# Third layer's end: the four sequences' ends in skewed stages, silu(z) loaded during the scan, x kept in DRAM, and the fourth layer's weights turned between the stages

## The chip, the cores and the metric

The kernel runs on one core of a Trainium2 chip. The core has five engines that work side by side, each on its own queue of instructions in order: TensorE (PE, matrix products, with a second queue PEld for loading the stationary operand), VectorE (DVE), ScalarE (ACT), GpSimd (POOL), and SyncE (SP), which here only starts DMA transfers. An engine waits for another through semaphores. On-chip memory is SBUF (128 partitions) and PSUM (where products land); DRAM is reached by DMA. The metric is the device time of one execution in microseconds, as the median of several runs.

## The reference

The program is a network of four different layers over an input of 4 sequences x 1024 tokens x 128 channels, all in one kernel. Every layer is of the form

```
xn = layernorm(x)
s  = mixer(xn)              # differs per layer
g  = silu(ffn(xn))          # differs per layer
x  = x + s * g
```

The change is at the end of the third layer and the start of the fourth. The third layer's mixer is a gated delta-rule scan with 16 heads. It makes from xn the projections z, x_gate, K and V, from a convolution of x_gate seven gates and the queries, and runs a recurrence over time. What follows the recurrence is this:

```
retrieved = einsum('blhsd,blhd->blhs', Y, Q) * sel_C_gate   # 16 heads x 2
y  = retrieved.reshape(b, l, 32) @ readout_w                # 32 -> 256
yf = y.reshape(b, l, 16, 16)                                # 16 groups of 16 channels
mean, var over (l, 16 channels of the group)                # group norm over all of a sequence
y  = (yf - mean) * rsqrt(var + 1e-5) * gn_w + gn_b
y  = y * silu(z)
y  = y + D_param * x_conv
out = residual + y @ out_w                                  # 256 -> 128
```

Its ffn is a mixture of eight experts. The fourth layer's mixer is causal attention with 16 heads of width 8 and relative position embeddings (`(q k + skewed(q e)) / sqrt(8)`, softmax, times v, `@ Wp.T + bp`), and its ffn is a SwiGLU with int8 weights divided by 127.

## The kernel before

**Frame.** x lives in one SBUF tile, `x_all` (128 tokens by partition, 4 x 8 tiles of tokens, 128 channels), from the first layer to the end of the third. `layer2` (L929-992; layers count from 0, so this is the third) writes the new x of each sequence to a DRAM tile `x3`, from which `layer3`, the fourth, reads.

**Third layer.** `norm(b)` normalises a sequence of x_all and stores it to DRAM (`xd`, L958). `project2` makes the projections; silu(z) goes to DRAM (`szd`), the residual with the D term already multiplied by out_w (`rd`) too, and the gate g of the experts (`gd`). `scan2` (L1382-1521) runs the recurrence in chunks. It is one stream of 64 steps on DVE with work of other kinds between the steps: `chunks2` makes four tables (`ktd`, `kdd`), one for each quarter of the steps, and each quarter fetches its part again from DRAM (`ktc`, `kdc`, `kt`, `qt`, L1297 and L1467-1469); the experts' work is interleaved with `next(beside)`.

**Its end.** `retrieve2` (L1523-1540) makes the transposed `retT`, 32 rows for each sequence. Then a loop goes over the four sequences (L983-992). For each: load silu(z), g and rd (L985-989), `out2`, then the update and the store. `out2` (L1542-1585): four products `py` of 32 rows by 512 columns (L1553), each copied to `y` by ACT (L1554), with DVE's statistics (L1555, L1556); two small products `pm` with a matrix of group means (L1563, L1567) with small DVE operations between (L1562-1566), a square root on ACT and four small DVE operations (L1570-1574); y scaled and shifted on DVE (L1576) and multiplied by silu(z) on POOL (L1577), 1024 columns at a time; 16 output products for each sequence in the program, 32 instructions in the trace (`po`, L1583), and two additions of `resid` on DVE (L1585). `k.update` (L225-228) then multiplies resid by g and adds it to x_all, both on POOL, for a whole sequence at once, and L992 stores the sequence to x3. Most tiles here have two buffers, so that the next sequence's loads and py products start while the current one ends.

**Fourth layer's start.** `load3` (L1602-1616) loads the weights; `prepare3` (L1628-1666) turns them: transposes of Wq, Wk, Wv, four transposes of a widened Wp with 16 DVE pieces (`WpB`, L1639-1644), eight transposes of the padded relative embeddings (`pad`, `emb`, L1650-1661), and the dequantised FFN weights (L1664). All of this stands in the program after the third layer and before `layer3` (L1672 on). `layer3` begins with sequence 0 alone: eight loads from x3 (L1809), layernorm (L136-143), transposes (L1824), products for q, k, v, and then a long pipeline of units in which scores, softmax and values of one unit lie between those of others. The scheduler is none other than the order of the program: each engine executes its instructions as written, and waits are put in from the tiles' uses.

## Time and profile before

| | us |
|---|---|
| median of 3 runs | 3265.0 (3252.33 to 3279.71) |
| profiled execution, device time | 3261.59 |
| its span | 3259.9 |
| mean granted TensorE clock | 0.734 of full speed |

The profiled execution is 3.4 us below the median; its span is 1.7 us shorter than its time. All times below are in microseconds from the span's start of that one execution. Where the stages lie:

| stage | from - to |
|---|---|
| last update of x by the second layer ends | 1277.1 |
| first store of normalised x (L958) | 1285.0 |
| first step of the scan | 1662 |
| fourth table's store leaves (L1378) | 1813.3 |
| loads of the last quarter's `ktc` leave (L1467, L1468) | 1826.8 - 1829.2 |
| last quarter of the scan begins | 1865 |
| last step of the scan | 2037 |
| first py product of sequence 0 | 2067.7 |
| last addition of resid, sequence 3, ends | 2153.5 |
| x3 store of sequence 3 leaves | 2158.8 |
| first load of the fourth layer leaves | 2161.6 |
| first normalisation in the fourth layer (L138) | 2168.3 |
| first comparison of scores in the fourth layer (L1986) | 2194.2 |
| end | 3259.9 |

The page gives each engine's busy time and count, then the span in 40 slices with busy tenths, the granted TensorE clock and the DMA traffic, and then groups of instructions by source line. A group's row has the busy time, the mean of one, the idle time of the engine just before, and what released it. The window rows cut the same data by stretches of time. In the timeline, a line has start, length, engine, source line, operation, tiles, shape and count, and in brackets the engine's idle time before it and who ended it. Rows with `q` behind the engine's name (SPq) are of its sequencer.

### The profile page before, as it was taken

Reading aid. Unit: us, or ns where it says so; the run is one execution under the profiler, and the core shown is the slowest. Engines: PE = TensorE matmul, PEld = TensorE weight load, DVE = VectorE, ACT = ScalarE, POOL = GpSimd, SP = SyncE. Lnnn points to the kernel's source line nnn. Section 1 sums busy time; section 2 is a strip of 40 time slices with the busy share of each in tenths; the row PEclk is TensorE's granted clock in tenths of the full one; section 3 lists DMA queues with packets and bytes.
Section 4 is the critical chain, followed back from the end, with each engine's and each line's share of the span. In section 5 each row is a group of like instructions: output and inputs, shape, how many; then the busy total and the mean of one; then the engine's idle time right before and its main releaser. Section 6 shows DMA issues by size and latency. Waiting matters only on the chain. (4 is left out here: it accounts for less than half of the span.)

```text
span 3259.9 us, 50636 instructions
## 1 busy us (share of the span) xinstructions
PE 2317.2 (71%) x18321; PEld 1327.2 (41%) x18321; DVE 2307.1 (71%) x5534; ACT 1487.5 (46%) x3248; POOL 1174.5 (36%) x1104
## 2 busy tenths in 40 slices
PE   5787777677776777965533772557888888888885
PEld 2555555222322323651101222344545555555553
DVE  5555545878878886657868878437678778777786
ACT  4555453433333334344322561125665665755663
POOL 3344334144444444224577222332322322323322
PEclk9888888678788888985555666566766766756676
DMA  3000000100000000320433444347677677766772
GB/s 89 3 1 1 1 1 1 35 0 0 0 0 1 0 0 33 105 84 0 111 95 105 109 108 99 110 119 209 187 213 207 181 209 217 202 195 193 200 231 71
DMA packets 396446, 303.46 MB, mean 93 GB/s; under 512 B 96272, under 2 KB 380812, under 8 KB 390564
## 3 DMA queue, kind: packets, MB, share of 16 engines
q1 hardware_dynamic: 395044, 296.03, 32.2%
q10 hardware_dynamic: 1152, 4.19, 0.4%
q8 instruction: 144, 2.36, 0.3%
q14 instruction: 106, 0.87, 0.1%
HBM read 160.63 MB, written 138.94 MB: 92 GB/s over the span
## 5 line engine op out<-in xcount | busy, mean ns | idle before, releaser
L2000 ACT ACTIVATE neg<-neg,low 128x640 f32<-128x640 f32 (+7 forms) x512 | 390.0, 763 | 153.9 <-DVE low L1993 153.8
L1945 POOL TENSOR_SCALAR_AFFINE_SELECT rel<-rel 128x512 f32<-128x512 f32 x288 | 179.9, 637 | 565.6 <-DMA rel<-flat 357.3
L1737 DVE STREAM_TRANSPOSE wT<-neg 128x640 f32<-128x640 f32 (+7 forms) x512 | 362.0, 753 | 7.6 <-ACT neg L2000 6.9
L1978 PE MATMUL score<-k,q 8*128 8x512 f32 (+3 forms) x1536 | 295.0, 747 | 91.2 <-DVE low L1993 91.0
L1993 DVE CUSTOM_DVE_ANT_0 neg<-score,rel,low 128x128 f32<-128x128 f32 (+3 forms) x448 | 217.5, 516 | 152.5 <-PE score L1978 105.6
L1914 PE MATMUL pr<-emb,q 8*128 8x256 f32 x1024 | 245.2, 569 | 45.0 <-ACT r L1916 27.2
L2014 PEld LDWEIGHTS po<-wT,vb 128*32 128x32 f32 x10240 | 208.1, 140 | 143.3 <-issue 78.0
L2014 PE MATMUL po<-wT,vb 128*32 128x64 f32 (+1 forms) x10240 | 242.9, 259 | 31.7 <-issue 17.3
L1914 PEld LDWEIGHTS pr<-emb,q 8*128 8x128 f32 x1024 | 153.6, 269 | 124.4 <-ACT r L1916 62.9
L1916 ACT COPY r<-pr 128x512 f32<-128x512 f32 x256 | 138.4, 581 | 144.2 <-PE pr L1914 95.1
L1993 DVE CUSTOM_DVE_ANT_0 neg<-score,rel 128x512 f32<-128x512 f32 (+3 forms) x320 | 149.3, 520 | 26.7 <-issue 15.4
L1978 PEld LDWEIGHTS score<-k,q 8*128 8x128 f32 x1536 | 103.0, 249 | 153.9 <-DVE low L1993 127.8
L835 PE MATMUL pg<-xnT,w 128*128 128x512 f32 x256 | 148.4, 663 | 7.7 <-DVE h L839 4.5
L214 PE MATMUL pt<-ident,three 128*24 128x128 bf16 x64 | 9.2, 295 | 201.9 <-DVE three L211 201.9
L788 POOL TENSOR_TENSOR prod<-rest,kv 128x2048 f32<-128x2048 f32 x32 | 145.6, 4599 | 18.4 <-ACT rest L778 18.4
L837 PE MATMUL pu<-xin,w 128*128 128x512 f32 x256 | 140.5, 632 | 14.3 <-DVE h L839 7.9
L826 PE MATMUL po<-h,w 128*128 128x512 f32 x256 | 129.6, 627 | 27.1 <-DVE h L839 27.1
L838 ACT ACTIVATE h<-pg 128x512 f32<-128x512 f32 x128 | 75.9, 595 | 156.2 <-PE pg L835 152.7
L1986 DVE TENSOR_SCALAR_CACHE_REDUCE neg<-score 128x384 f32<-128x384 f32 (+2 forms) x192 | 79.7, 415 | 69.3 <-PE score L1978 69.3
L1050 PE MATMUL ph<-xin,upT 128*128 128x512 bf16 (+1 forms) x128 | 71.3, 588 | 78.5 <-DVE xin L1044 77.7
L1455 PE MATMUL read<-kt,const_sb 128*128 128x128 f32 x256 | 50.1, 366 | 94.2 <-POOL kt L1450 94.2
L431 PE MATMUL px<-hT,xbcT 128*128 128x512 f32 x256 | 115.4, 595 | 0.0
(621 smaller groups left out, 5690.5 us busy)
## 6 DMA issues: line engine op xcount, KB each, us to landing
flat<-r SPq DMA_DIRECT2D x256, 256.0 KB
rel<-flat SPq DMA_DIRECT2D x112, 512.0 KB
flat<-r SPq DMA_DIRECT2D x256, 128.0 KB
rel<-flat SPq DMA_DIRECT2D x96, 256.0 KB
kt<-kd SPq DMA_DIRECT2D x16, 512.0 KB
qt<-qd SPq DMA_DIRECT2D x16, 512.0 KB
kdc<-kdd SPq DMA_DIRECT2D x16, 512.0 KB
ktc<-ktd SPq DMA_DIRECT2D x16, 512.0 KB
```

Source lines behind the costliest of these rows:

```text
L788: nc.gpsimd.tensor_tensor(prod, attn.rearrange("p (t h g) -> p t h g", t=4, g=16)[:, t].unsqueeze(2).to_broadcast(each), kv[:, t, 1, :].re ...
L826: nc.tensor.matmul(po, W["w2"][:, e, c, :], h[:, c, :], start=(e == 0 and c == 0), stop=(e == 7 and c == 1))
L835: nc.tensor.matmul(pg, W["w1"][:, e, c * P : (c + 1) * P], xnT, start=True, stop=True)
L837: nc.tensor.matmul(pu, W["w3"][:, e, c * P : (c + 1) * P], xin, start=True, stop=True)
L1737: nc.vector.transpose(weights[at, pair][j][:, t % 2, 0 : (t + 1) * P], S[j][:, 0 : (t + 1) * P])
L1914: nc.tensor.matmul(to[:, m, :], q[at, t * P : (t + 1) * P], W["emb"][at, i, :], start=True, stop=True)
L1916: nc.scalar.copy(r[:, n], to)
L1945: nc.gpsimd.affine_select(out=rel[:, :, slot(back), :], in_=rel[:, :, slot(0), :], compare_op=op, fill=fill, base=0, pattern=[[0, 4], [-si ...
L1978: nc.tensor.matmul(sc[:, j, 0 : last - first], q[at(j), 1 + t * P : 1 + n], kk[at(j), first:last], start=True, stop=True)
L1993: nc.vector.tensor_tensor_reduce(out=neg[:, begin:last], in0=sc[:, j, begin - first : last - first], in1=rel[:, j, slot : slot + (last - b ...
L2000: nc.scalar.activation(neg[:, 0:n], neg[:, 0:n], AF.Exp, bias=here, scale=-1.0, accum_out=group["sums"][:, j, t : t + 1])
L2014: nc.tensor.matmul(o[32 * j : 32 * j + 32, 2 * pair + m.start : 2 * pair + 2, :], vb[:, kb, j].rearrange("p a d -> p (a d)"), weights[j][: ...
```

## The change

The end of the third layer is rewritten, and four things are moved.

- **x by way of DRAM.** `norm(b)` also stores x_all to a new DRAM tile `xr`. After the gates are made, x_all's room is given up (`whole.close()`), and a pool for the fourth layer's turned weights is opened in its place. Each sequence's end loads its x from xr into one of two buffers.
- **silu(z) during the scan.** The tiles of `chunks2` are in pools of their own. Once the four tables are made, `behind_tables()` closes these, opens a pool with four silu(z) tiles in their room, and issues their loads (1 MB each) on SP.
- **The ends in stages.** The loads of resid and g for all four sequences, and of the fourth layer's weights, stand ahead of `retrieve2`. `out2` is a generator with four stages: py and statistics; group statistics; scaling, product with silu(z), load of x; output products, additions, update and store. A loop runs them skewed: in round n sequence b is at stage n - b, for sequence 0 first.
- **Weights turned between.** `prepare3` is a generator too, and one of its steps follows each stage.
- **Engines.** Scaling y goes from DVE to ACT; the product with silu(z) for the second 128 of the 256 channels from POOL to DVE; resid times g from POOL to DVE. The addition to x stays on POOL. Both go by half a sequence now, and so does the store to x3.

The order of instructions in `layer3` is unchanged on every engine. The diff:

```diff
--- before.py
+++ after.py
@@ -926,14 +926,17 @@
     nc.scalar.activation(W["ldt"], W["ldt"], AF.Exp)
 
 
-def layer2(k, W, x_all, eps5, ps, banks, x3):
+def layer2(k, W, x_all, eps5, ps, banks, x3, whole, last, I):
 
     nc, tc = k.nc, k.tc
     tokens = lambda b: slice(b * NT, (b + 1) * NT)
     with tc.tile_pool(name="l2", bufs=1) as keep, tc.tile_pool(name="l2dram", bufs=1, space=DRAM) as dram:
         wide = lambda name: dram.tile([P, NB * NT, D], F32, tag=name, name=name)
 
-        xd, rd, gd = wide("xd"), wide("rd"), wide("gd")
+        xd, rd, gd, xr = wide("xd"), wide("rd"), wide("gd"), wide("xr")
         szd = dram.tile([P, 2, NB * T], F32, tag="szd", name="szd")
 
         kd = dram.tile([NT, NB, 16, 16, P], F32, tag="kd", name="kd")
@@ -954,6 +957,7 @@
 
                 def norm(b):
 
+                    nc.sync.dma_start(out=xr[:, tokens(b), :], in_=x_all[:, tokens(b), :])
                     var, rs = k.layernorm(p2, x_all[:, tokens(b), :], xn[:, tokens(b), :], eps5)
                     nc.sync.dma_start(out=xd[:, tokens(b), :], in_=xn[:, tokens(b), :])
                     ms = p2.tile([P, NT], F32, tag="ms", name="ms")
@@ -972,24 +976,48 @@
             experts = experts2(k, W, f1, f2, ps, xd, gd)
             with tc.tile_pool(name="l2m", bufs=1) as mp:
                 gates2(k, W, mp, ps, raw, cosp, sinp, outg, coef, experts)
+        whole.close()
+        t3 = last.enter_context(tc.tile_pool(name="t3", bufs=1, side="right"))
+        room, szs = ExitStack(), []
+        tp1 = room.enter_context(tc.tile_pool(name="l2t", bufs=1, side="right"))
+        tp2 = room.enter_context(tc.tile_pool(name="l2td", bufs=2, side="right"))
+        def behind_tables():
+            room.close()
+            pre = room.enter_context(tc.tile_pool(name="l2pre", bufs=1, side="right"))
+            for b in range(NB):
+                szs.append(pre.tile([P, 2, T], F32, tag=f"sz{b}", name="sz"))
+                nc.sync.dma_start(out=szs[b], in_=szd[:, :, b * T : (b + 1) * T])
         with late, tc.tile_pool(name="l2s1", bufs=1) as p1, tc.tile_pool(name="l2s", bufs=2) as p2, \
                 tc.tile_pool(name="l2sd", bufs=2, space=DRAM) as dram2:
-            scan2(k, p1, p2, ps, dram2, kd, qd, coef, o, experts)
+            scan2(k, p1, p2, ps, dram2, kd, qd, coef, o, experts, tp1, tp2, behind_tables)
         banks.close()
         ps = PsumTags(banks, tc, {"mm": 4, "tr": 2, "o": 2}, "ps2o")
-        with tc.tile_pool(name="l2o", bufs=2) as p2:
-            retT = p2.tile([P, T], F32, tag="retT", name="retT")
-            retrieve2(k, p2, ps, o, cosp, sinp, outg, retT)
+        with room, tc.tile_pool(name="l2o", bufs=NB) as p4, tc.tile_pool(name="l2x", bufs=2) as p2, \
+                tc.tile_pool(name="l2r", bufs=1) as p1, tc.tile_pool(name="w3", bufs=1) as w3:
+            parts = []
             for b in range(NB):
-                sz = p2.tile([P, 2, T], F32, tag="szb", name="szb")
-                nc.sync.dma_start(out=sz, in_=szd[:, :, b * T : (b + 1) * T])
-                g = p2.tile([P, NT, D], F32, tag="g", name="g")
+                resid, g = (p4.tile([P, NT, D], F32, tag=tag, name=tag) for tag in ("resid", "g"))
+                nc.sync.dma_start(out=resid, in_=rd[:, tokens(b), :])
                 nc.sync.dma_start(out=g, in_=gd[:, tokens(b), :])
-                resid = p2.tile([P, NT, D], F32, tag="resid", name="resid")
-                nc.sync.dma_start(out=resid, in_=rd[:, tokens(b), :])
-                out2(k, W, p2, ps, b, retT, sz, resid, eps5)
-                k.update(x_all[:, tokens(b), :], resid, g)
-                nc.sync.dma_start(out=x3[:, tokens(b), :], in_=x_all[:, tokens(b), :])
+                parts.append((resid, g))
+            W3 = load3(k, w3, I)
+            turned = prepare3(k, t3, W3, ps)
+            retT = p1.tile([P, T], F32, tag="retT", name="retT")
+            retrieve2(k, p1, ps, o, cosp, sinp, outg, retT)
+            ends = [
+                out2(k, W, p4, p2, ps, b, retT, szs[b], *parts[b], eps5, xr[:, tokens(b), :], x3[:, tokens(b), :])
+                for b in range(NB)
+            ]
+            for n in range(2 * NB):
+                for b in range(NB):
+                    if 0 <= n - b:
+                        next(ends[b], None)
+                        next(turned, None)
+            drain(turned)
+        return W3
 
 
 def experts2(k, W, p1, p2, ps, xd, gd):
@@ -1379,7 +1407,7 @@
         yield ktd, kdd
 
 
-def scan2(k, p1, p2, ps, dram, kd, qd, coef, o, beside):
+def scan2(k, p1, p2, ps, dram, kd, qd, coef, o, beside, tp1, tp2, behind_tables):
 
 
 
@@ -1387,7 +1415,7 @@
     nc = k.nc
     v = nc.vector
     whole = p1.tile([P, 512 // CH], F32, tag="whole", name="whole")
-    tables = chunks2(k, p1, p2, ps, dram, kd, coef, whole)
+    tables = chunks2(k, tp1, tp2, ps, dram, kd, coef, whole)
     made = []
 
     def table():
@@ -1515,6 +1543,9 @@
                     table()
             while c == NC - 6 and len(made) < min(4, i + 2):
                 table()
+            if behind_tables and len(made) == 4:
+                behind_tables()
+                behind_tables = None
     for i in (NT - 2, NT - 1):
         drain(made_of[i])
     drain(beside)
@@ -1539,7 +1570,7 @@
     k.transpose_tiles(ps, "tr", tiles, retT)
 
 
-def out2(k, W, p2, ps, b, retT, sz, resid, eps5):
+def out2(k, W, p2, px, ps, b, retT, sz, resid, g, eps5, x_from, x_to):
 
     nc = k.nc
     y = p2.tile([P, 2, T], F32, tag="y", name="y")
@@ -1554,6 +1585,7 @@
             nc.scalar.copy(y[:, c, tok], py)
             nc.vector.bn_stats(st[:, c, half, :], y[:, c, tok])
         nc.vector.bn_aggr(mv[:, c, :], st[:, c])
+    yield
     mean, var = mv[:, :, 0], mv[:, :, 1]
     pm = ps.tile([P, 4], F32, tag="o", name="pm")
     flat = p2.tile([P, 4], F32, tag="flat", name="flat")
@@ -1572,17 +1604,26 @@
     nc.vector.tensor_tensor(scale, scale, W["gnw"], ALU.mult)
     nc.vector.tensor_tensor(shift, scale, pm[:, 0:2], ALU.mult)
     nc.vector.tensor_tensor(shift, W["gnb"], shift, ALU.subtract)
+    yield
     for c in range(2):
-        nc.vector.tensor_scalar(y[:, c, :], y[:, c, :], scale[:, c : c + 1], shift[:, c : c + 1], op0=ALU.mult, op1=ALU.add)
-        nc.gpsimd.tensor_tensor(y[:, c, :], y[:, c, :], sz[:, c, :], ALU.mult)
+        nc.scalar.activation(y[:, c, :], y[:, c, :], AF.Identity, bias=shift[:, c : c + 1], scale=scale[:, c : c + 1])
+    nc.gpsimd.tensor_tensor(y[:, 0, :], y[:, 0, :], sz[:, 0, :], ALU.mult)
+    nc.vector.tensor_tensor(y[:, 1, :], y[:, 1, :], sz[:, 1, :], ALU.mult)
+    x = px.tile([P, NT, D], F32, tag="x", name="x")
+    nc.sync.dma_start(out=x, in_=x_from)
+    yield
     for half in range(2):
         po = ps.tile([P, 4, D], F32, tag="o", name="po")
         for t in range(4):
             at = (4 * half + t) * P
             for c in range(2):
                 nc.tensor.matmul(po[:, t, :], y[:, c, at : at + P], W["outw"][:, c, :], start=(c == 0), stop=(c == 1))
-        r = resid[:, 4 * half : 4 * half + 4, :]
-        nc.vector.tensor_tensor(r, r, po, ALU.add)
+        part = slice(4 * half, 4 * half + 4)
+        nc.vector.tensor_tensor(resid[:, part], resid[:, part], po, ALU.add)
+        nc.vector.tensor_tensor(resid[:, part], resid[:, part], g[:, part], ALU.mult)
+        nc.gpsimd.tensor_tensor(x[:, part], x[:, part], resid[:, part], ALU.add)
+        nc.sync.dma_start(out=x_to[:, part], in_=x[:, part])
+    yield
 
 
 
@@ -1626,11 +1667,13 @@
 
 
 def prepare3(k, w, W, ps):
     nc = k.nc
     new = lambda name, shape: w.tile(shape, F32, tag=name, name=name)
     for name in ("Wq", "Wk", "Wv"):
         W[name + "T"] = new(name + "T", [P, D])
         k.transpose_tiles(ps, "tr", [W[name]], W[name + "T"])
+        yield
 
     W["WpB"] = new("WpB", [P, 4, 4, D])
     with k.tc.tile_pool(name="wide3", bufs=1) as rp:
@@ -1642,6 +1685,7 @@
             nc.tensor.transpose(pt, wide[:, i].rearrange("p j a d -> p (j a d)"), k.ident)
             for a in range(4):
                 nc.vector.tensor_scalar(W["WpB"][:, i, a, :], pt, k.c("of_a")[:, a : a + 1], None, op0=ALU.mult)
+            yield
     W["bpw"] = new("bpw", [P, D])
     nc.gpsimd.tensor_copy(W["bpw"], W["bp"])
     W["emb"] = new("emb", [P, 4, 256])
@@ -1653,6 +1697,7 @@
                 nc.gpsimd.tensor_copy(spread(pad[:, c, :])[:, i], heads_of(W["rel"][:, c, :])[:, i])
         for i in range(4):
             k.transpose_tiles(ps, "tr", [pad[:, c, i * P : (i + 1) * P] for c in (0, 1)], W["emb"][:, i, :])
+            yield
 
         e0 = rp.tile([P, 4], F32, tag="e0", name="e0")
         nc.vector.tensor_copy(e0, W["emb"][:, :, 0])
@@ -1664,6 +1709,7 @@
             nc.vector.tensor_scalar(f, W[name], 1.0 / 127.0, None, op0=ALU.mult)
             W[name + "T"] = new(name + "T", [P, 3, D])
             k.transpose_tiles(ps, "tr", [f[:, c, :] for c in range(3)], W[name + "T"].rearrange("p c d -> p (c d)"))
+            yield
 
 
 ORDER3 = (7, 0, 6, 1, 5, 2, 4, 3)
@@ -2087,7 +2133,7 @@
     xp = whole.enter_context(tc.tile_pool(name="x", bufs=1, side="right"))
     x_all = xp.tile([P, NB * NT, D], F32, tag="x_all", name="x_all")
 
-    right = ExitStack()
+    right, last = ExitStack(), ExitStack()
     w1 = right.enter_context(tc.tile_pool(name="w1", bufs=1, side="right"))
     with tc.tile_pool(name="w0", bufs=1) as w0, ExitStack() as st:
         ps = PsumTags(st, tc, {"mm": 4, "tr": 2, "o": 2}, "ps0")
@@ -2113,14 +2159,9 @@
             st2 = ExitStack()
             ps = PsumTags(st2, tc, {"mm": 4, "tr": 2, "o": 2}, "ps2")
         with st2:
-            layer2(k, W2, x_all, eps5, ps, st2, x3)
-    w3 = right.enter_context(tc.tile_pool(name="w3", bufs=1, side="right"))
-    W3 = load3(k, w3, I)
-    with whole, right, tc.tile_pool(name="t3", bufs=1) as t3, ExitStack() as st:
+            W3 = layer2(k, W2, x_all, eps5, ps, st2, x3, whole, last, I)
+    with last, ExitStack() as st:
         ps = PsumTags(st, tc, {"sc": 1, "tr": 3, "o": 1}, "ps3")
-        prepare3(k, t3, W3, ps)
-        right.close()
-        whole.close()
         layer3(k, W3, x3, out, eps5, ps)
 
 
```

## The prediction

> **What bounds the kernel now.** I read the page first. TensorE and VectorE are equally loaded over the whole span, and neither is full, so the page alone decides nothing about one stage.
>
> ```profile
> PE 2317.2 (71%) x18321; PEld 1327.2 (41%) x18321; DVE 2307.1 (71%) x5534; ACT 1487.5 (46%) x3248; POOL 1174.5 (36%) x1104
> PEclk9888888678788888985555666566766766756676
> ```
>
> One slice is 81.5 us. The change lies in slices 26 and 27, where the granted clock is 0.5 to 0.6. Next I cut that time into stages: last scan reads and loads; the four sequences' ends (L1542-1585); the update of x and the turning of layer 3's weights; layer 3's start; layer 3's bulk.
>
> ```profile
> 2050.00:2068.00 18.00, 9.55 (x49) 8.82 (x50) 6.77 (x8) 1.44 (x3) 4.57 (x3) 0.69 0.84 292
> 2068.00:2153.00 85.00, 53.59 (x176) 37.23 (x175) 36.44 (x73) 10.93 (x21) 34.40 (x15) 0.57 0.21 68
> 2153.00:2166.00 13.00, 5.55 (x24) 4.15 (x24) 9.94 (x34) 1.66 (x5) 7.90 (x18) 0.74 0.24 78
> 2166.00:2209.00 43.00, 28.01 (x104) 18.59 (x104) 3.46 (x23) 18.20 (x34) 8.69 (x8) 0.61 0.78 216
> ```
>
> Columns: PE, PEld, DVE, ACT, POOL busy, clock, DMA share, GB/s. In the second row no engine is full: 53.6 us of PE in 85. The waits of that stretch say why:
>
> ```profile
> PEld po L1583 <- POOL y L1577: 22.9, 8, 6.0
> PE po L1583 <- POOL y L1577: 18.4, 8, 5.9
> PEld pm L1567 <- DVE flat L1566: 14.2, 4, 5.6
> ```
>
> PE idles in each sequence for its statistics and for its product with silu(z), because each sequence ends before the next gets through. Third sequence, in order of time:
>
> ```profile
> 2120.29 0.58 PE L1567 MATMUL pm<-flat,const_sb 128*128 128x2 f32 x2 [5.52 <-DVE flat L1566]
> 2123.70 4.99 POOL L1577 TENSOR_TENSOR y<-y,szb 128x1024 f32<-128x1024 f32 x2 [3.47 <-DVE y L1576]
> 2128.74 6.24 PE L1583 MATMUL po<-outw,y 128*128 128x128 f32 x28 [1.08 <-POOL y L1577]
> 2135.01 0.69 DVE L1585 TENSOR_TENSOR resid<-resid,po 128x512 f32<-128x512 f32 x1 [2.14 <-PE po L1583]
> 2135.78 2.34 POOL L227 TENSOR_TENSOR resid<-resid,g 128x1024 f32<-128x1024 f32 x1 [7.10 <-DVE dev L1564]
> 2135.80 2.33 DVE L1565 TENSOR_TENSOR dev<-dev 128x2 f32<-128x2 f32 x1
> ```
>
> The last two lines matter: a DVE product of 128x2 takes 2.33 us beside POOL's product, and 0.16 us alone (least of that row), ending with POOL's. The sequences' last residual additions end at 2095.27, 2115.38, 2135.70 and 2153.47: 20.1, 20.3 and 17.8 us apart, 85.8 us from the first py matmul (2067.65). Then the way into layer 3:
>
> ```profile
> 2154.00 2.35 POOL L227 TENSOR_TENSOR resid<-resid,g 128x1024 f32<-128x1024 f32 x1
> 2156.43 2.34 POOL L228 TENSOR_TENSOR x_all<-x_all,resid 128x1024 f32<-128x1024 f32 x1
> 2161.56 3.65 SPq L1809 DMA_DIRECT2D x<-x  x8
> 2168.29 0.30 ACT L138 ACTIVATE ln_rs<-ln_mv,eps 128x8 f32<-128x8 f32 x1 [3.41 <-DVE ln_mv L137]
> ```
>
> From 2153.47 to the first normalisation of layer 3 at 2168.29 there are 14.8 us, in which nothing but POOL's update, the store, eight loads and the weights' turning happens. The weights' turning runs beside them, so the chain is the update's.
>
> **The change, part by part.**
>
> *The ends in stages.* I add PE's own work in the new order, as the built kernel has it. All 16 py products stand ahead of the first output product. Here 12 of them took 9.06+2.07+5.48 = 16.6 us, 1.38 each, so 16 take 22.1. Four pairs of pm at 0.58 add 2.3, and the turnings of Wq, Wk, Wv and of four wide tiles 2.1 (seven at about 0.3). The first output product comes 26.5 us after the first py (before: 18.8). After it come 128 output products (28.6 us in the window), pads' and FFN weights' transposes (2.2 + 2.4), four pm pairs (2.3) and the last residual addition (0.7). PE's sum is 62.7 us. Above it stand the waits that staging does not cover. Last sequence alone, from second pm to output product, was 5.6 us in the third sequence; in the new order the third sequence's output products (7.15 us) lie beside it. The uncovered part is 0 if every small DVE operation is alone, and about 9 if one of them in each sequence waits out a POOL product (4 x 2.2). I take the middle, 4.5: in the row of before three of four waited, but then POOL's products were twice as long. The stage takes 67.2 us instead of 85.8: 18.6 less, bounds 14 to 23.
>
> *Moves between engines in it.* y's scaling goes from DVE (two of 0.77) to ACT. ACT was busy 10.9 of 85 us and a copy of 128x512 took 0.59, so two of about 1.1; the first lies on the chain with +0.3, taken as part of the 4.5. One half of y times silu(z) goes from POOL (2.5) to DVE (1024 columns, twice the 0.68 of L1537: 1.3), parallel to POOL's half, and resid times g from POOL (2.34) to DVE (two of 0.68). DVE gains 4 x (1.3 + 1.4 - 1.5) = 4.8 us on 36.4 + 9.9; it has 67, so it stays below. If it stops being covered, that is 5 us.
>
> *The way into layer 3.* New: resid times g 0.68, x plus resid of half a sequence on POOL 1.17, store 0.32, three load issues 1.3 (five stand in front of the last store, and they no longer wait for its landing, since only the first sequence is read), and from the last issue's end to ln_rs 3.1 as before. That is 6.6, plus 1 for one DVE product behind a POOL one: 7.5 (6.6 to 9). It was 14.8: 7.3 less. What now waits in a queue: on DVE a sequence's residual additions (for its output products) stand ahead of the next one's product with silu(z), which is in the order summed above; on SP the third x load waits, and only later stores and layer 3's loads are behind it. The turning (9.9 us of DVE, 5.5 of PE) goes into the stage above and is in its sum.
>
> *x by DRAM.* Four stores of 512 KB ahead of the first normalised x's store. x was complete at 1277.1, that store left at 1285.0, and DMA moved 1 GB/s between: nothing on the path. If that cover were gone, four times 512 KB at the 223 GB/s shown below, 9 us. Four loads on SP: the third and fourth wait for the store of the sequence two before, 20 us ahead of their use: nothing, else one landing (2 to 3 us) each.
>
> *silu(z) during the scan.* Four loads, 4.2 MB, on SP ahead of the ktc loads of the scan's fourth block. The ktc loads left at 1826.8 to 1829.2; the block starts near 1865, and DMA stood still from 1840 to 1850:
>
> ```profile
> 1840.00:1850.00 10.00, 9.90 (x19) 2.34 (x19) 8.66 (x26) 8.78 (x19) 1.42 (x2) 0.60 0.00 0
> 1857.00:1866.00 9.00, 3.08 (x27) 2.89 (x26) 7.41 (x28) 1.42 (x5) 3.59 (x3) 0.95 1.03 223
> ```
>
> At 223 GB/s they take 19 us, and 2.1 MB of ktc 9 more: from 1818 to about 1846, some 15 us early. Cost 0; bounds -1 (the z loads gone from 2051) and +20: if all of it leaves only at 1829 and runs at half the rate, ktc is there at 1885. At 2051 the same 4.2 MB leave as before (eight loads of resid and gate instead of two sequences' z, gate and resid), so layer 3's weights behind them come no later.
>
> *Sum.* 18.6 + 7.3 = 25.9. Layer 3's instructions keep their order, so the earlier start is passed on. From the profiled execution's 3261.6 us: 3235.7. The median of the three runs is 3.4 above that execution, so I set 3237.
>
> **The rivals.**
>
> *DVE behind POOL.* Twelve products with two SBUF operands move to DVE, and POOL's remaining 12 run beside them. If each waits out a POOL operation, 12 x 2.2 = 26 us, of which 4.5 are in the sum: 22 of the 26 us come back, 3258. For it: 3 of the 4 L1565 took over 0.2 us. Against: POOL gives up 4 x (2.5 + 2.3) us of 34. The same result comes if all py and the turnings, ahead of the first output product, only delay it. The Trainium skill, "SBUF — State Buffer", section "Who interferes with whom", says that a DVE instruction with two SBUF inputs contends with a GpSimd instruction that reads SBUF, the one issued first holding the port for its whole length. The 2.33 against 0.16 us agrees. Chance of a gain of 0 to 15 us: 0.22.
>
> *PE warm.* With fewer pauses the granted clock goes up. Output products and transposes at 1.0 instead of 0.5 halve 28.6 + 4.6: 16.6 less; DVE's 51 us are then near: gain 42, 3219. For: in the bulk of layer 3 PE runs at 0.69. Against: from 2068 to 2086 PE had hardly a pause and the clock stayed at 0.50. The Trainium skill, "TensorE: Matmul & The Clock Gate", section "Part 1: The HAM clock gate", puts full clock after about 3.4 us of sustained work; by it this rival would be the forecast, and those 18 us (py products use 32 rows) differ from it. Chance 0.22.
>
> *Layer 3 slower (the other side).* Its 1050 us run at a granted clock that moves between stretches of the same work (0.63 at 2209-2300, 0.69 over 2209-2900, PE busy 589 of 691 us). A shifted start could shift that mean. One hundredth of clock is 0.85 x 1050 / 69 = 13 us, so from 0.02 it decides against the change, and 0.05 gives 3237 + 65 = 3302. For: the medians' runs spread by 27 us. Against: the instructions are the same. Chance 0.06.
>
> *It doesn't do what it says.* If stages do not overlap since queues hold them in order, only the way into layer 3 is shorter by 7.3: 3254. PE's and DVE's queues of the built kernel are interleaved, so 0.04 beside the first rival.
>
> **How the numbers follow.** The forecast, gain 19 to 32, has 0.46, 3230 to 3243. About 1%, 33 us, is what a measurement of this kernel can tell from no change. Faster by over 1%: the warm case (0.22) and, with the runs' spread, a quarter of the forecast (0.12): 0.34. Slower by over 1%: most of the third rival and of an unseen cost, 0.06. Within: 0.60. The range takes the warm case down to 3214 and the contended cases up to 3260; the layer-3 rival and half of the ends stay out.
>
> **What would show it.** Right: sequences' last residual additions about 34 us after the first py and then about 11 apart; the output products of one sequence right behind the other's; 7 to 8 us from the last of them to ln_rs; L1467's loads landed before 1860 and scan steps at the same times. Wrong: scan steps later than before from the fourth block on (silu(z) loads); DVE products of two SBUF tiles at 2 us and more (first rival); a clock of over 0.7 in the stage (second); or the gain there at layer 3's first score but not at the end of the kernel (third).

## The result, and the profile after

The changed kernel took 3238.6 us (median of 6 runs, 3232.4 to 3246.5), the kernel before 3269.2 us (6 runs, 3252.3 to 3279.7): a recorded ratio of 0.9917, 95% interval 0.9897 to 0.9937 (it is not the quotient of the two medians). The forecast was 3237 us. In a second set of rounds the medians were 3241.4 and 3263.5, ratio 0.9924 (0.9900 to 0.9947). The profiled execution took 3233.7 us with a span of 3231.9, 28.0 less than before.

The page of the changed kernel, the two lines that were shown of before:

```profile
PE 2318.6 (72%) x18321; PEld 1316.4 (41%) x18321; DVE 2302.6 (71%) x5538; ACT 1498.5 (46%) x3256; POOL 1157.2 (36%) x1100
PEclk9888888688778878995555665566766766767776
```

All engines do the same work as before, to within 1.5%. What changed is when. Time by stage, in the profiled executions:

| stage | before | after | difference |
|---|---|---|---|
| start to the scan's last step | 2037.5 | 2032.3 | -5.2 |
| from there to the first py product | 30.1 | 29.7 | -0.4 |
| first py to the last addition of resid ("the ends") | 85.8 | 68.3 | -17.5 |
| from there to the fourth layer's first normalisation ("the way in") | 14.8 | 7.9 | -6.9 |
| from there to the first comparison of scores | 25.9 | 27.0 | +1.1 |
| from there to the end | 1065.7 | 1066.7 | +1.0 |

The ends, the way in, the start of the fourth layer and its bulk in the window view (PE, PEld, DVE, ACT, POOL busy, clock, DMA share, GB/s):

```profile
2062.00:2130.30 68.30, 54.64 (x201) 34.16 (x200) 45.42 (x107) 22.36 (x34) 22.93 (x24) 0.67 0.24 80
2130.30:2138.20 7.90, 0.00 (x0) 0.00 (x0) 3.75 (x17) 0.03 (x1) 5.62 (x5) 0.74 0.42 136
2138.20:2165.20 27.00, 21.94 (x81) 14.01 (x82) 0.37 (x2) 12.57 (x26) 4.14 (x4) 0.63 0.65 159
2165.20:2865.00 699.80, 587.16 (x8504) 367.67 (x8501) 525.00 (x1666) 425.61 (x990) 196.29 (x281) 0.69 0.69 202
```

PE is busy for 54.6 of the 68.3 us of the ends, where it was 53.6 of 85.0. POOL fell from 34.4 to 22.9. In the way in PE does nothing at all: the turning is gone from there. PE's rows of the changed kernel's ends, in order of time:

```profile
2062.00 9.06 PE L1584 MATMUL py<-retT,ro 32*128 32x512 f32 x14
...
2071.98 2.07 PE L1584 MATMUL py<-retT,ro 32*128 32x512 f32 x2
...
2087.10 5.49 PE L1584 MATMUL py<-retT,ro 32*128 32x512 f32 x6
2092.52 5.77 PE L1620 MATMUL po<-outw,y 128*128 128x128 f32 x32
2102.30 0.35 PE L1595 MATMUL pm<-flat,const_sb 128*128 128x2 f32 x2 [4.01 <-DVE flat L1594]
...
2105.41 3.97 PE L1620 MATMUL po<-outw,y 128*128 128x128 f32 x28
...
2116.35 0.90 PE L123 MATMUL pt<-const_sb,fup 128*128 128x128 f32 x3 [6.64 <-DVE fup L1709]
...
2125.07 0.71 PE L1620 MATMUL po<-outw,y 128*128 128x128 f32 x4 [1.89 <-POOL y L1610]
2126.15 3.39 PE L1620 MATMUL po<-outw,y 128*128 128x128 f32 x28 [0.37 <-DVE y L1611]
```

Up to the first output product at 2092.52 PE never waits. After it the brackets count 4.0 + 6.6 + 1.9 + 0.4 = 12.9 us of waiting. The output products of sequence 0 came out as 5.77 us, and those of the others in less; before it was 7.2 for each. The last update, and the way into the fourth layer:

```profile
2131.70 1.26 POOL L1624 TENSOR_TENSOR x<-x,resid 128x512 f32<-128x512 f32 x1 [0.63 <-DVE resid L1623]
2132.99 0.34 SPq L1625 DMA_DIRECT2D x<-x  x1
2133.37 1.41 SPq L1855 DMA_DIRECT2D x<-x  x3
2138.17 0.30 ACT L138 ACTIVATE ln_rs<-ln_mv,eps 128x8 f32<-128x8 f32 x1 [14.49 <-DVE ln_mv L137]
```

Behind the last store, three of eight loads are left, and they leave at once. Before, POOL's two operations were 4.7 us long, and the first load left 2.75 us after the store.

### The profile page after: what moved, and what is told of

Read it like the earlier page. It is cut to its first block, busy times and chain, and to the rows that moved or that the text cites. A ratio compares the mean times of both kernels' runs of the same rounds, so it can differ in the third digit from the quotient of the medians.

```text
span 3231.9 us, 50643 instructions
## 1 busy us (share of the span) xinstructions
PE 2318.6 (72%) x18321; PEld 1316.4 (41%) x18321; DVE 2302.6 (71%) x5538; ACT 1498.5 (46%) x3256; POOL 1157.2 (36%) x1100
## 5 line engine op out<-in xcount | busy, mean ns | idle before, releaser
L1960 PE MATMUL pr<-emb,q 8*128 8x256 f32 x1024 | 240.6, 555 | 44.5 <-ACT r L1962 28.6
L837 PE MATMUL pu<-xin,w 128*128 128x512 f32 x256 | 141.0, 634 | 13.8 <-DVE h L839 7.8
```

The source lines that it names most:

```text
L837: nc.tensor.matmul(pu, W["w3"][:, e, c * P : (c + 1) * P], xin, start=True, stop=True)
L1960: nc.tensor.matmul(to[:, m, :], q[at, t * P : (t + 1) * P], W["emb"][at, i, :], start=True, stop=True)
```

## The experiments

All stage lengths below are read like those of the table. Times of single executions come with the note that the part behind the first scores alone differs by up to 17 us between executions (see the last section), so the stages carry the verdicts. In the runs made from the changed kernel the turning of the weights lies in the ends (but for "turning last"), in those made from the kernel before it lies in the way in; where the two kinds are compared, ends and way in are taken together: 100.6 us before, 76.2 changed.

| run | scan's last step | ends | way in | first score to end | span |
|---|---|---|---|---|---|
| before | 2037.5 | 85.8 | 14.8 | 1065.7 | 3259.9 |
| before again | 2035.8 | 85.8 | 14.8 | 1069.6 | 3262.1 |
| changed | 2032.3 | 68.3 | 7.9 | 1066.7 | 3231.9 |
| changed again | 2030.6 | 68.3 | 7.9 | 1063.4 | 3227.0 |
| no skew | 2032.0 | 81.7 | 7.5 | 1065.7 | 3242.3 |
| turning last | 2029.5 | 63.2 | 11.4 | 1076.0 | 3236.0 |
| silu(z) late | 2032.2 | 68.3 | 7.9 | 1063.5 | 3228.6 |
| before, halves | 2038.1 | 78.7 | 13.8 | 1073.4 | 3260.6 |
| engines back | 2032.7 | 84.1 | 8.5 | 1065.4 | 3246.1 |
| before, tables apart | 2031.7 | 84.8 | 15.2 | 1066.4 | 3252.9 |
| py together | 2033.3 | 54.9 | 7.7 | 1080.7 | 3233.3 |
| resid times g back | 2032.4 | 76.9 | 7.9 | 1066.3 | 3239.4 |
| scaling and silu(z) products back | 2033.3 | 81.6 | 7.6 | 1068.9 | 3246.9 |
| py together, WpB on ACT | 2030.5 | 54.2 | 7.7 | 1065.4 | 3213.2 |

**The kernel before, once more.** No edit.

> The kernel before, unchanged, once more. It asks whether the scan's last step, 5.2 us earlier in the changed kernel's execution (2032.3 against 2037.5), belongs to the change. Theory (nothing in the scan was on its path, so this is how one execution differs from the next): the last step lands anywhere from 2030 to 2045 here, differing from 2037.5 by 2 us or more. Rival (the silu(z) pools and the new order speed up the scan): 2037.5 within 1 us again. Both: 85 to 87 us from the first py to the last residual addition, and 14 to 15.5 from there to the fourth layer's first normalisation.

The ends and the way in repeat to 0.1 us. The last step came at 2035.8, between the two expectations: 1.7 us earlier, all of it from before the scan's first step. So two executions do differ by that much, but the changed kernel's 2032.3 was not yet explained.

**Without the skew.**

```diff
-for n in range(2 * NB):
-    for b in range(NB):
-        if 0 <= n - b:
-            next(ends[b], None)
-            next(turned, None)
+for b in range(NB):
+    for n in range(5):
+        next(ends[b], None)
+        next(turned, None)
```

> The changed kernel, but the four sequences' ends run one after another; the weights are still turned between the stages, and all moves between engines stay. Theory (the gain of the stage comes from PE working on the next sequence while the statistics and the product with silu(z) of one are made): the pauses return, less what the engine moves and halves took out, and the stage from the first py to the last residual addition takes 77 us (73 to 84) against 68.3; the way into the fourth layer stays at 7 to 9; the time is 5 to 15 us above the changed kernel's. Rival (the engine moves alone made the gain): 71 us or less in the stage.

81.7 us: within the range, above its middle. Undoing the skew makes the ends 13.4 us longer, against a gain of 17.5, so the engine moves alone did not make the gain. With the way in it is 89.2, so 11.4 of the 24.5 us are left without the skew. What the run undoes is the order from the statistics on: in its trace all py products still stand ahead of the first output product, which comes 29.3 us after the first py.

**Engines as before, skew kept.**

```diff
-        nc.scalar.activation(y[:, c, :], y[:, c, :], AF.Identity, bias=shift[:, c : c + 1], scale=scale[:, c : c + 1])
-    nc.gpsimd.tensor_tensor(y[:, 0, :], y[:, 0, :], sz[:, 0, :], ALU.mult)
-    nc.vector.tensor_tensor(y[:, 1, :], y[:, 1, :], sz[:, 1, :], ALU.mult)
+        nc.vector.tensor_scalar(y[:, c, :], y[:, c, :], scale[:, c : c + 1], shift[:, c : c + 1], op0=ALU.mult, op1=ALU.add)
+        nc.gpsimd.tensor_tensor(y[:, c, :], y[:, c, :], sz[:, c, :], ALU.mult)
...
-        nc.vector.tensor_tensor(resid[:, part], resid[:, part], g[:, part], ALU.mult)
+        nc.gpsimd.tensor_tensor(resid[:, part], resid[:, part], g[:, part], ALU.mult)
```

> The changed kernel with the engines of before in the ends: scaling y on DVE, both products with silu(z) and resid times g on POOL; skew, halves, turning and x by DRAM as changed. POOL then has 4 x (2 x 2.5 + 4 x 1.3) = 41 us in the stage. Theory (the skew made most of the gain, and the moves unload POOL): the stage takes 71 to 77 against 68.3, the way in 8.5 to 10 against 7.9. Rival (DVE's two-operand products behind POOL cost what the moves save): stage 69 or less.

84.1 us, far outside both. "The skew made most of the gain" falls with it. With the way in, which the turning has left, it is 92.6: skew, halves and turning gain 8.0 of the 24.5 us when the engines are as before. DVE's and POOL's rows say why:

```profile
2084.83 5.08 POOL L1610 TENSOR_TENSOR y<-y,sz 128x1024 f32<-128x1024 f32 x2 [17.16 <-DVE y L1609]
2096.70 0.69 DVE L1621 TENSOR_TENSOR resid<-resid,po 128x512 f32<-128x512 f32 x1 [4.28 <-PE po L1619]
2097.47 1.27 POOL L1622 TENSOR_TENSOR resid<-resid,g 128x512 f32<-128x512 f32 x1 [7.56 <-DVE resid L1621]
...
2099.83 2.47 DVE L1609 TENSOR_SCALAR y<-y,scale,shift 128x1024 f32<-128x1024 f32 x2
2101.84 1.59 POOL L1623 TENSOR_TENSOR x<-x,resid 128x512 f32<-128x512 f32 x1
2103.39 4.63 POOL L1610 TENSOR_TENSOR y<-y,sz 128x1024 f32<-128x1024 f32 x2
```

Two queues tie the sequences to each other here. On DVE, the scaling of the second sequence's y (L1609) stands behind the residual additions of the first (L1621), and these wait for the first sequence's output products, the first of them with 4.28 us of idle time. The scaling's operands were made by 2091.3; it began at 2099.83. On POOL, the second sequence's product with silu(z) stands behind the first one's update: POOL is idle for 7.56 us, but in that time the product could not have run either, since its y was not scaled. The first half of y was scaled by 2100.64 and its product began at 2103.39, so POOL's queue adds 2.7 us to DVE's 8. PE's next output products then wait for POOL. So the sequences run nearly in lockstep, whatever the order in the program. In the changed kernel the scaling is on ACT, which has no residual additions: the second sequence's first product with silu(z) began at 2094.43, ahead of the first addition to x. (The part on the kernel before says that engines run the program in its written order. That is not exact: in the program this product stands behind the first sequence's additions to x, and other instructions below stand elsewhere than the text has them. By which rule the built queue is ordered was not followed.)

**Which of the moves.** Two runs: resid times g alone back on POOL, and scaling and products with silu(z) alone back (edits as the two parts of the last diff).

> The changed kernel with resid times g back on POOL, by halves; the rest as changed. Both the run without skew (81.7) and the one with all engines as before (84.1) lost nearly the whole gain of the stage (85.8 to 68.3), so skew and engine moves need each other. Theory (POOL's queue is what ties sequences together: there the next sequence's product with silu(z) stands behind the update of the one before, which waits for its output products; the longer the update on POOL, the later the next output products): POOL gets 8 x 1.3 = 10 us more, stage 72 to 79. Rival (only the products with silu(z) matter): 70 or less.

> The changed kernel with the scaling of y back on DVE and both halves' products with silu(z) back on POOL; resid times g stays on DVE. In the built kernel the second sequence's products stand on POOL behind the first sequence's two additions to x, while in the changed kernel they stand ahead of them. Theory (as for the run beside this one: POOL's queue ties the sequences): stage 74 to 82. Rival (only resid times g matters): 70 or less.

76.9 and 81.6 us, 8.7 and 13.4 more than in the changed kernel. Both times are in that theory's ranges, and both rivals fall, but the traces show POOL's queue as the tie only in part. With resid times g back, the products of the third and fourth sequence are held by POOL's updates for 1.4 and 2.3 us after their y is scaled; the rest of the 8.7 was not followed. With scaling and products back, the second sequence's product waits for DVE's scaling:

```profile
2102.95 5.09 POOL L1610 TENSOR_TENSOR y<-y,sz 128x1024 f32<-128x1024 f32 x2 [0.69 <-DVE y L1609]
```

Its scale and shift were made by 2092.0, and DVE began the scaling at 2101.4, behind the first sequence's residual additions and products with g. So there it is DVE's queue. Scaling and products with silu(z) were not moved back one without the other, so how the 13.4 us divide between them is open.

**Weights turned last.** `next(turned, None)` is taken out of the loop, so that `drain(turned)` does it all.

> The changed kernel, but the fourth layer's weights are turned after all four ends instead of between their stages. Theory: they were never on the path before, where POOL's update took as long, but with the update short they would be: the stage gets 4 to 8 us shorter (62 to 64 against 68.3), the way into the fourth layer 6 to 9 longer (14 to 17 against 7.9), the time 0 to 4 us above the changed kernel's. Rival (turning between the stages is hidden at no cost, so it is worth its whole 12 us): stage unchanged at 68, way in 18 to 21.

Ends 63.2 as expected, way in 11.4, better than expected: together 74.6 against the changed kernel's 76.2. Turning between the stages gains nothing here; it is 1.6 us worse than this order. ("Last" holds for the text alone: in the trace Wq, Wk, Wv and the four wide pieces are turned among the output products, from 2086.6 to 2108.5.) The way in of this run:

```profile
2122.40:2133.90 11.50, 2.62 (x13) 1.52 (x13) 10.21 (x30) 1.04 (x4) 5.00 (x4) 0.74 0.19 63
```

DVE is busy for 10.2 of 11.5 us there: the turning and the fourth layer's statistics are the chain. Of the 10.2 us, 3.5 are one copy of 128x4 (L1702), which takes 3.55 us beside a POOL MEMSET that ends with it; in the changed kernel the same copy takes 0.17.

**silu(z) loaded late.** The loads of `behind_tables()` are issued after `load3` instead.

> The changed kernel, but silu(z) is loaded after the scan, behind the fourth layer's weights, and not during it. Theory (the loads were hidden anyway, since the first product with silu(z) comes 24 us after the first py): stage 68 to 69, the time within 2 us of the changed kernel's beyond what two executions differ by, and the scan's fourth quarter not earlier. Rival (prefetching is part of the gain): the first product with silu(z) waits for its load, stage 71 or more.

Ends, way in and scan are the changed kernel's to 0.1 us. But this run does not load silu(z) behind the scan. The built queue has the loads far ahead of where the text has them:

```profile
1827.67 1.91 SPq L1007 DMA_DIRECT2D sz<-szd  x3
1876.83 0.60 SPq L1007 DMA_DIRECT2D sz<-szd  x1
```

Three leave some 12 us later than in the changed kernel, right behind the ktc loads, and the fourth some 59 us later; the scan ends at 2032. So the run shows that this shift costs nothing. What loading behind the scan would cost, and with it what the prefetch is worth, was not tested.

**The update by halves, alone, in the kernel before.**

```diff
-                k.update(x_all[:, tokens(b), :], resid, g)
-                nc.sync.dma_start(out=x3[:, tokens(b), :], in_=x_all[:, tokens(b), :])
+                for half in range(2):
+                    ...
+                    nc.vector.tensor_tensor(resid[:, part], resid[:, part], g[:, part], ALU.mult)
+                    nc.gpsimd.tensor_tensor(x_all[:, at], x_all[:, at], resid[:, part], ALU.add)
+                    nc.sync.dma_start(out=x3[:, at], in_=x_all[:, at])
```

> The kernel before with one part of the change: resid times g on DVE, the addition to x and the store to x3 by halves of a sequence; everything else as before (sequences one after another, weights turned after them). Theory (the update and the turning each took about the same time behind the last residual addition, and turning keeps DVE for some 10 us, so shortening the update alone uncovers the turning, as the run with the turning last showed with 11.4): the way into the fourth layer goes from 14.8 to 11 to 13.5, the stage from 85.8 to 82 to 86. Rival (the update alone was the chain, so that this edit alone is worth the prediction's 7.3): way in 7 to 9.

Way in 13.8 (a little above the range): the shorter update alone is worth 1.0 us there, since DVE's copies for the turning now lie between the fourth layer's statistics (2157.1 to 2159.4). So the prediction's 7.3 us are not the update's alone. The turning out of the way with the long update was not run. The ends took 78.7, below the range: with resid times g off POOL, 7.2 us go there without any skew. Ends and way in together are 92.5, so this small edit alone gains as much as skew, halves and turning together do with the old engines (92.6).

**Tables in pools of their own, in the kernel before.**

```diff
-    tables = chunks2(k, p1, p2, ps, dram, kd, coef, whole)
+    tables = chunks2(k, tp1, tp2, ps, dram, kd, coef, whole)
```

> The kernel before, with only the tiles of chunks2 in pools of their own, as the changed kernel has them. In four executions of the changed scan its last step came at 2029.5 to 2032.3, in two of before at 2035.8 and 2037.5. Theory (the pools do nothing; the difference comes from the changed order and from when PE's clock rises): last step at 2035 to 2038.5. Rival (apart from each other, the tables' tiles wait less for each other): 2033 or earlier.

2031.7: the theory fell, and the time is the rival's. The scan's gain in the changed kernel comes from the tables' own pools, and neither from silu(z) nor from x in DRAM: all eleven executions with these pools end the scan at 2029.5 to 2033.3, the three without at 2035.8 to 2038.1. The rival's reason, fewer waits, does not show. From 1500 us to the last step, in the kernel before and in this run:

```profile
1500.00:2037.86 537.86, 261.28 (x741) 102.01 (x740) 427.16 (x834) 206.32 (x426) 258.38 (x184) 0.60 0.39 95
1500.00:2031.97 531.97, 265.69 (x739) 104.40 (x739) 422.19 (x833) 205.66 (x424) 258.42 (x184) 0.59 0.40 98
```

DVE's idle time is 110.7 and 109.8 us, its busy time 427.2 and 422.2 (426.1 in the second execution of before): 4.0 to 5.0 us less, for the same operations. The 28 additions to the tables (KT from KT and more) alone take 43.8 us instead of 46.6. The first step comes 5.6 us later than in before and the steps then take 11.4 us less. Why the operations are shorter was not followed.

**py side by side.** The changed kernel with one function ahead of the stages:

```diff
+    for c in range(2):
+        for half in range(2):
+            tok = slice(half * 512, (half + 1) * 512)
+            pys = [ps.tile([P, 512], F32, tag="mm", name="py") for b in range(NB)]
+            for b in range(NB):
+                rows = slice(32 * b, 32 * b + 32)
+                nc.tensor.matmul(pys[b], W["ro"][rows, c * P : (c + 1) * P], retT[rows, tok], start=True, stop=True)
+            for b, (y, st, mv) in enumerate(parts):
+                nc.scalar.copy(y[:, c, tok], pys[b])
+                nc.vector.bn_stats(st[:, c, half, :], y[:, c, tok])
```

> The changed kernel, but the py products of the four sequences are made first, the four sequences' products of the same columns next to each other (each uses other 32 of PE's 128 rows), four PSUM tiles at a time; skew from the group statistics on. In the changed kernel's trace a py alone takes 2.07, while neighbours of two sequences start 0.16 to 0.17 apart and run at the same time. Theory (products on different rows run side by side, so PE's 26.6 us of py fall to about 9, and ACT's 16 copies at 0.59 and DVE's 16 statistics at 0.68 set the pace): the last py copy 12 us after the first py, the first output product 18 to 22 after it instead of 30.5, the stage 48 to 58 instead of 68.3, the time 10 to 20 below the changed kernel's. Rival (they do not, or the output products wait for POOL and DVE all the same): stage 64 or more.

Ends 54.9, in the theory's range; the first output product comes 22.0 us after the first py. Median 3219.9 of 6 runs against 3263.3 for before, ratio 0.9852 (0.9815 to 0.9889). PE's rows:

```profile
2062.96 2.09 PE L1588 MATMUL py<-retT,ro 32*128 32x512 f32 x8
2065.71 9.03 PE L1588 MATMUL py<-retT,ro 32*128 32x512 f32 x24 [0.66 <-ACT y L1590]
```

Eight instructions (four py, one for each sequence) take 2.09 us, as long as the two of one py alone in the changed kernel. All 16 py need 11.1 us of PE instead of 26.6. In the second row four of them take 2.75 us, as PE and ACT pass the four PSUM tiles back and forth: 2.05 of these are ACT's four copies.

**The changed kernel again, and a version that is faster than it and than before.** The last run adds to py side by side:

```diff
-                nc.vector.tensor_scalar(W["WpB"][:, i, a, :], pt, k.c("of_a")[:, a : a + 1], None, op0=ALU.mult)
+                nc.scalar.activation(W["WpB"][:, i, a, :], pt, AF.Identity, scale=k.c("of_a")[:, a : a + 1])
```

> The changed kernel, unchanged, once more, in the rounds of the next run, for comparing both on one chip. All theories: stage 67.5 to 69, way in 7.5 to 8.5, scan's last step 2029 to 2033; ratio to the kernel before 0.988 to 0.994. If two executions of the same kernel differ by more than 5 us, the difference lies behind the fourth layer's first scores and not in the scan or the ends.

> The changed kernel with the py products of the four sequences side by side (as in the run before, stage 54.9), and the 16 pieces of WpB scaled by ACT instead of DVE, which was busy 46.7 of those 54.9 us. Theory (DVE's queue sets the pace there): DVE loses 16 x 0.34 = 5.5 us, stage 49 to 54, time 17 to 27 us below the changed kernel's. Rival (the pace is set by POOL's products and PE's clock): stage 54 to 58, time 12 to 20 below.

On one chip: before 3263.5 us (11 runs), changed 3241.4 (6 runs, ratio 0.9924, 0.9900 to 0.9947), this version 3217.6 (4 runs, ratio 0.9862, 0.9846 to 0.9878). Its ends took 54.2 us, 0.7 less than with DVE's pieces, so by the stage the rival is right that DVE was not what set the pace; that POOL's products and PE's clock do was not shown. The time, 23.8 us below the changed kernel's, lies in the theory's range and above the rival's, but against before this version is no faster than py side by side alone (0.9862 and 0.9852). The changed kernel repeated its stages; its two executions differ by 4.9 us in span, 1.8 of them in the scan and 3.3 behind the first scores.

## Why the prediction was right, and where its terms were not

The sum said 25.9 us, the profile shows 28.0, the two sets of medians 30.6 and 22.1. That the total comes so near is in part luck: the two terms of the sum gave 24.4 us, the stages up to the first py added 5.6 that no term had, and 2.1 were lost behind the first normalisation. Term by term:

- **The ends: 67.2 predicted, 68.3 measured.** Two errors cancelled in it. Ahead of the first output product PE took 30.5 us and not 26.5, because a py was put at the mean of a stretch of before (1.38) in which two sequences' products ran at the same time; alone it is 2.07. Behind it stood 37.8 us and not 40.7: the output products took 20.1 us and not 28.6, and PE's waits 12.9 and not 4.5. The last residual additions came 37.0 us after the first py and then 13.2, 11.7 and 6.4 apart, where 34 and about 11 were named. The largest wait, 6.6 us for `fup`, is none of those that the prediction named: a dequantisation of the FFN weights stood on DVE behind products that were held up, and the weights' transposes stood ahead of the last sequence's statistics on PE.
- **What carries it.** The step "waits go since the next sequence's work lies beside" is right only together with the engine moves. The prediction costed the moves as DVE's load and a shorter chain; their larger use is that the next sequence's scaling no longer stands behind the residual additions in DVE's queue, nor, to a smaller part, its product with silu(z) behind the update in POOL's (ends and way in: before 100.6, engines back 92.6, no skew 89.2, changed 76.2).
- **The way in: 7.5 predicted, 7.9 measured**, by the steps that were listed. That it needs the turning out of the way was in the sum (the turning was counted in the stage), and the two runs with the turning in the way in show it: 13.8 and 11.4.
- **silu(z) and x by DRAM: 0 and 0**, as predicted. The silu(z) loads left at 1815.7 to 1818.2, the ktc loads of the fourth block behind them at 1825.4 to 1827.7, and that block's first product came at 1865.5, 4.1 us earlier than before and 0.9 later than with the tables' pools alone; it waited for no load. No addition to x waited for its load from xr. (The part on the kernel before has the scan wrong in one point: it has 128 steps in eight blocks of 16, a table serves block i and block i + 4, and the fourth block, called the last quarter there, begins at 1869.7 and not at 1865. The cover was 5 us larger than the prediction took it.)
- **The step that was missed** is that chunks2's tiles went into pools of their own. The prediction read this part of the diff as a place for silu(z) and gave it no term; it is worth some 4 to 6 us at the scan's last step, as the run with that edit alone showed.
- **The earlier start is passed on**: the fourth layer is 30.1 us earlier at its first normalisation, 29.0 at the first comparison of scores, 28.0 at the end.

The rivals. *DVE behind POOL* happens, by more than 0.5 us on five of the twelve products. In the changed kernel one of them:

```profile
2108.50 2.85 DVE L1623 TENSOR_TENSOR resid<-resid,g 128x512 f32<-128x512 f32 x1
```

Alone it takes 0.68. Over the eight L1623 and four L1611 the excess is 4.1 + 2.2 = 6.3 us, against the 26 that all of them would give. *PE warm* came true in part: the clock rose with the output products, which saved 8.5 us, but waits took the time, so the ends did not get shorter by it. *Layer 3 slower* did not show in the changed kernel (1066.7 and 1063.4 us behind the first scores, before 1065.7 and 1069.6); see below. *It doesn't do what it says* is excluded by the rows above.

## What to carry to other kernels

When stages of independent pieces are skewed, look at every engine's queue for the instruction of the next piece that stands behind a wait of the piece before: an engine that does both (here DVE, with the scaling behind the residual additions, and POOL) ties them together, and then the skew gains little alone. Read the built queue in the trace: an edit of the text may not move an instruction to where the text has it, and then the run tests something else. A mean duration from a stretch where instructions run side by side is not the cost of one alone; take the row of an instance that has no such neighbour. Cost every line of a diff, also one that only moves tiles into other pools.

## What the runs showed of the hardware

**A busy PE whose clock stays low.** In the changed kernel:

```profile
2062.00:2092.00 30.00, 30.00 (x48) 11.61 (x47) 16.34 (x50) 13.00 (x22) 3.59 (x6) 0.50 0.30 95
2096.00:2100.00 4.00, 2.29 (x18) 2.10 (x17) 3.48 (x8) 0.00 (x0) 2.11 (x3) 0.93 0.00 0
```

PE had no pause for 30 us and was granted 0.50; those are nearly all py products, on 32 of 128 rows. Some 4 us after output products with 128 rows began, at 2092.5, the clock was 0.93, though PE was less busy. The Trainium skill, "TensorE: Matmul & The Clock Gate", section "Part 1: The HAM clock gate", gives about 3.4 us of sustained activity for this; the second row agrees with it and the first does not. That the number of rows makes the difference is one reading, and no run here changed it alone. Against rows in use speaks the run with py side by side, where four such products fill 128 rows at once: PE was busy for 11.1 of the 11.8 us from 2062.96, and the clock was 0.50 there too. What decides stays open.

**Products on different rows run at the same time.** Four py of four sequences took 2.09 us, one alone 2.07. The Trainium skill, "TensorE: Matmul & The Clock Gate", section "Part 3: Packing small matmuls — row/col tiling", reports 3.07 times for four tiles of 32 rows and 512 columns; here the first four py came out at 4 times, all 16 at 2.4 (26.6 / 11.1), with PE waiting for the copies in between.

**The same fourth layer, 1063 to 1081 us.** Its instructions are the same in all of these runs, and from the first scores to the end it took 1063.4 to 1080.7 us. It goes with the granted clock in part. Here the first 1050 us behind the first scores of the changed kernel's second execution, and of the one with py side by side:

```profile
2163.63:3213.63 1050.00, 867.18 (x13327) 543.40 (x13325) 809.04 (x2557) 632.10 (x1484) 290.46 (x416) 0.70 0.68 197
```

```profile
2152.56:3202.56 1050.00, 873.96 (x12984) 549.36 (x12981) 799.64 (x2533) 625.15 (x1468) 290.12 (x416) 0.67 0.68 197
```

0.70 with 1063.4 us and 0.67 with 1080.7, so between these two about 6 us for each hundredth; the third rival had put 13. The other executions do not all fit: before and its run with halves both had 0.68, and took 1065.7 and 1073.4. Whether the start's time has a part in it stays open: the executions in between do not order themselves by it (early starts at 2147.8 and 2152.6 gave 1065.4 and 1080.7). A spread of 17 us is of the size by which the profile's 28 us and the medians' 22 and 31 differ.
